# Layer 1 of a two-layer graph network: attention in fewer, larger interleaving steps, masks copied by ScalarE

## The chip, the cores and the metric

The kernel runs on one core of one Trainium2 chip. The metric is the device time in microseconds from the first to the last instruction of one execution. A core has five engines that run their own queues in order and meet at semaphores: TensorE (PE for matmuls, PEld for its weight loads), VectorE (DVE), ScalarE (ACT), GpSimd (POOL) and SyncE (SP, which here only starts transfers). Matmul results land in PSUM[...]; everything else lives in SBUF.

## The reference

32 graphs of 512 nodes with 256 features pass two layers, each a graph part and a feed-forward part with a layer norm ahead and a residual around it. Only layer 1's graph part is touched by the change. With `adj` of zeros and ones it is a four-head attention over the neighbours:

```python
h = jnp.einsum('bnd,hde->bhne', nodes_embed, W)
e_src = jnp.einsum('bhne,hte->bhtn', h, a_src)
e_dst = jnp.einsum('bhne,hte->bhtn', h, a_dst)
...
weight = weight + mask * (e_src[:, :, t, :, None] + e_dst[:, :, t, None, :])
weight = jax.nn.leaky_relu(weight, negative_slope=0.01)
weight = jnp.where(node_adj[:, None] == 0, NEG, weight)
attention = jax.nn.softmax(weight, axis=-1)
dst = jnp.einsum('bhij,bhje->bhie', attention, h) + bias[None, :, None, :]
out = jax.nn.relu(dst) + h
```

then a layer norm per head over 64 features. Its feed-forward part soft-assigns the nodes to 64 slices per head, runs a small bidirectional state-space mixer (`_hydra`) over the 64 slice tokens, and spreads the result back to the nodes.

## The kernel before

**Layer 0** (`layer0_sorted`, up to about 2540 us) does its graph convolution and feed-forward part. Near its end it already runs the first lines of layer 1: constants, and the masks of sequence 0 (L1093).

**Layer 1** (`layer1_plain`, L850) has two streams of work, both written as Python generators whose `yield` ends a step.

- The *attention* stream, `attentions` (L1292): for each sequence `b` it interleaves `attention(b)` with `prepare(b + 1)` through `woven` (L65), which takes steps of the two in proportion to the counts it is given.
- The *mixer* stream, `mixer` (L1557), for a pair of sequences: `slices` twice (logits `lgp` L1319, `exp` and the soft assignment `sw` on ScalarE and VectorE L1320 to L1326, the gathered tokens `yTp` L1331, the transposes `swp` L1336), `tokens`, `scan` (the state-space chain, `xp` L1384 to `vp` L1541), and `unslice` twice (`outp` L1551, added to `x` at L1553).

Each `yield` of the mixer names a wish (4, 7, 2 ...; 68 for a pair), and the loop at L1575 gives the attention stream `want * PACE` steps of credit for it. `PACE` (L881) follows from `TURNS` (steps of `attention`) and `STEPS` (steps of `prepare`). `slices` also pulls the attention stream until its own sequence has been attended (L1305). The order of these steps is the order in which instructions are given out; the framework plans each engine's queue from it.

`prepare(b)` gathers the rows (L1139), makes the mask (`masks`, L1058), normalises (`normed`), transposes (`turned`), projects each tile of 128 nodes (`hp`, L1165) with three exponentials and a copy on ScalarE (L1168 to L1171), adds the bias on GpSimd (L1174), and sends the nodes' own terms through DRAM to get them broadcast over partitions (`own`, L1185). A mask of one tile is made in `turn` (L1066): four bf16 transposes into a PSUM tile `maskp` and one copy to uint8 (L1070). Outside the start-up these PSUM tiles share a pool of four banks (`any`) with `hp`, `lgp`, `yTp`, `swp`, `outp` and the scan; four more banks (`pv`) hold the attention's sums.

`attention(b)` runs over four tiles `j` of neighbours and two head pairs `q`. A turn `(q, j)` is: `weigh` two turns ahead, that is two VectorE instructions L1198 (maximum of two exponentials, times the mask) into the `att` buffers; two matmuls `avp` (L1231), whose two heads stand side by side in TensorE's columns; and, when `q` is the second pair, four matmuls `adp` (L1238) for the softmax's denominators. Each turn ends a step. In between, pieces of `norm(b - 1)` (L1266), the head-wise layer norm of the sequence before, are run as steps of their own (L1241). At the end the sums are copied, transposed and divided (L1246 to L1261).

Of the kernel before, what the change touches and what calls it, by code (L numbers as in the profile page):

```python
# [18 lines left out]
P = 128  # L19
N = 512  # L20
D = 256
NT = N // P
# [42 lines left out]
def woven(a, na, b, nb):  # L65

    done_a = done_b = 0
    a, b, end = iter(a), iter(b), object()
    while a is not None or b is not None:
        if b is None or (a is not None and done_a * nb <= done_b * na):  # L70
            done_a += 1
            if next(a, end) is end:
                a = None
        else:
            state = next(b, end)
            if state is end:
                b = None
            elif state is True and a is not None:

                if next(a, end) is end:  # L80
                    a = None
            elif state is True:
                yield True
                continue
            if state is not True:
                done_b += 1
        yield
# [9 lines left out]
def layer0_sorted(tc, ident, eps, x, adj, w, x2s, ranks, over, following):  # L97
# [13 lines left out]
    CAPS = [24, 9, 7, 6, 5, 5, 5] + 5 * [4] + 4 * [3] + 7 * [2] + 9 * [1]  # L111
    STEPS = [16, 12, 9, 8, 7, 6, 5, 4, 3, 2, 1, 0]
    NC = len(STEPS)
    LEAD = 16
# [735 lines left out]
def layer1_plain(tc, ident, eps, x2s, ranks, adj, w, out, over, ps):  # L850
# [3 lines left out]
    nc = tc.nc  # L854
# [16 lines left out]
    SLOPE = 0.01  # L871
    HE = HO + 1
    AP = AH // 2
    TURNS = AP * NT + 6
    STEPS = 15
    WANTED = 68
    AHEAD = 2
    ATT = 2 * (AHEAD + 2) + AP + 1
# [1 line left out]
    AHEAD_X = 2 * GB + 1  # L880
    PACE = 1.04 * GB * (TURNS + STEPS) / WANTED  # L881

# [3 lines left out]
    with ExitStack() as ctx:  # L886
# [169 lines left out]
        masked = {}  # L1056

        def masks(b, bank="any"):  # L1058

            a, raw = [], []  # L1060

            def load(t):
                raw.append(se.tile([P, N], I32, tag="ai", name=f"ai{b}_{t}", bufs=2))
                nc.sync.dma_start(raw[t], adj[b, t * P : (t + 1) * P, :])

            def turn(t):  # L1066
                pt = ps.tile([P, NT, P], BF16, tag=bank, name=f"maskp{b}_{t}")
                for j in range(NT):
                    nc.tensor.transpose(pt[:, j, :], a[t][:, j * P : (j + 1) * P], identb)
                nc.vector.tensor_copy(mask[:, :, t * P : (t + 1) * P], pt)  # L1070

            load(0)
            load(1)
            yield
            for t in range(NT):
                n = b * NT + t
                a.append(se.tile([P, N], BF16, tag="a", name=f"a{b}_{t}", bufs=3))
                nc.scalar.activation(a[t], raw[t], AF.Identity, accum_out=edges[:, 0, n : n + 1])
                nc.scalar.activation(raw[t], raw[t], AF.Square, accum_out=edges[:, 1, n : n + 1])
                if t + 2 < NT:  # L1080
                    load(t + 2)
                if t == 1:
                    mask = se.tile([P, NT, N], mybir.dt.uint8, tag="mask", name=f"mask{b}")
                    yield
                if t > 1:
                    turn(t - 2)
                    yield
            for t in range(NT - 2, NT):
                turn(t)
                yield  # L1090
            masked[b] = mask

        yield from masks(0, "mm")  # L1093
# [39 lines left out]
        def prepare(b):  # L1133

            while b >= AHEAD_X and b - AHEAD_X not in stored:
                yield True
            xt = xs[b] = sb.tile([P, NT, D], F32, tag="x", name=f"x{b}", bufs=AHEAD_X)
            for t in range(NT):
                nc.gpsimd.indirect_dma_start(  # L1139
                    out=xt[:, t, :], out_offset=None, in_=x2s[b // SEG],  # L1140
                    in_offset=bass.IndirectOffsetOnAxis(
                        ap=ranks[:, b * NT + t : b * NT + t + 1].bitcast(U32), axis=0))

            hv = sb.tile([P, NT, AH, HE], F32, tag="hv", name=f"hv{b}")
            xn = hv.rearrange("p t h e -> p (t h e)")[:, : NT * D].rearrange("p (t d) -> p t d", t=NT)
            edged = masks(b) if b not in masked else range(3)
            for i, _ in enumerate(edged):
                if i < 3 or b not in masked:
                    yield
                if i == 2:  # L1150
                    normed(xt, xn, f"c{b}")
                    nc.gpsimd.tensor_add(xt, xt, beta.unsqueeze(1).to_broadcast([P, NT, D]))
                    yield
            mask = masked.pop(b)
            xnT = yield from turned(xn, "x3T", f"x3T{b}")
            yield


            ht = sb.tile([P, NT, AH * HO], F32, tag="ht", name=f"ht{b}")
            other = sb.tile([P, NT, AH], F32, tag="other", name=f"other{b}")  # L1160
            mine = sb.tile([P, AH, NT], F32, tag="mine", name=f"mine{b}")
            for t in range(NT):
                ph = psum("any", f"hp{b}_{t}")
                for c in range(DC):
                    nc.tensor.matmul(ph[:, : AH * (HO + 2)], xnT[:, c, t * P : (t + 1) * P], wa[:, c, :],  # L1165
                                     start=c == 0, stop=c == DC - 1)
                d = ph[:, AH * HO : AH * HO + AH]
                nc.scalar.activation(mine[:, :, t], ph[:, AH * (HO + 1) : AH * (HO + 2)], AF.Exp, scale=1.0 - SLOPE)  # L1168
                nc.scalar.activation(hv[:, t, :, HO], d, AF.Exp)
                nc.scalar.activation(other[:, t, :], d, AF.Exp, scale=SLOPE - 1.0)  # L1170
                nc.scalar.copy(ht[:, t, :], ph[:, : AH * HO])  # L1171
                yield

            nc.gpsimd.tensor_add(hv[:, :, :, :HO], ht.rearrange("p t (h e) -> p t h e", h=AH),  # L1174
                                 abias.rearrange("p (h e) -> p h e", h=AH).unsqueeze(1).to_broadcast([P, NT, AH, HO]))
            yield
            pt = psum("any", f"minep{b}")
            nc.tensor.transpose(pt[: AH * NT, :P], mine.rearrange("p h t -> p (h t)"), ident)
            row = sb.tile([AH * NT, P], F32, tag="turned", name=f"turned{b}", bufs=1)
            nc.scalar.copy(row, pt[: AH * NT, :P])  # L1180
            own_row = dr.tile([AH, N], F32, tag="own", name=f"ownd{b}")
            nc.sync.dma_start(own_row.rearrange("h (t p) -> (h t) p", p=P), row)
            own = [wide("own", f"own{b}_{h}", AH + 2) for h in range(AH)]
            for h in range(AH):
                nc.sync.dma_start(own[h], own_row[h].partition_broadcast(P))  # L1185
            for t in range(NT):
                nc.vector.tensor_mul(hv[:, t, :, :HO], hv[:, t, :, :HO], hv[:, t, :, HO:].to_broadcast([P, AH, HO]))
            ready[b] = mask, ht, hv, other, own
            yield
# [11 lines left out]
        def attention(b):  # L1201

            mask, ht, hv, other, own = ready[b]
# [19 lines left out]
            for i, (q, j) in enumerate(turns):  # L1223
                if i + AHEAD < len(turns):
                    begin(b, i + AHEAD)
                elif b + 1 in ready:
                    begin(b + 1, i + AHEAD - len(turns))

                for k in range(2):
                    h = 2 * q + k  # L1230
                    nc.tensor.matmul(pv[q][k * HO : (k + 1) * HO, :], hv[:, j, h, :HO], weighed[b, h, j],  # L1231
                                     start=j == 0, stop=j == NT - 1)

                if q + 1 == AP:
                    if j == 0:
                        pd = psum("pv", f"adp{b}")
                    for h in range(AH):
                        nc.tensor.matmul(pd[h * HW : (h + 1) * HW, :], hv[:, j, h, HO:].to_broadcast([P, HW]),  # L1238
                                         weighed.pop((b, h, j)), start=j == 0, stop=j == NT - 1)
                yield  # L1240
                if unfinished and i != 2:  # L1241
                    next(unfinished[0], None)
                    yield
                    if i > 2:
                        unfinished.pop()
            dT = wide("att", f"adT{b}", ATT)  # L1246
            nc.scalar.copy(dT, pd)
            vT = [wide("att", f"avT{b}_{q}", ATT) for q in range(AP)]
# [15 lines left out]
        unfinished = []  # L1264
# [27 lines left out]
        def attentions():  # L1292
            yield from prepare(0)
            for b in range(B):
                nxt = prepare(b + 1) if b + 1 < B else iter(())
                yield from woven(attention(b), TURNS - 4, nxt, STEPS)
            for _ in unfinished[0]:
                yield

# [924 lines left out]
```

## Time and profile before

The time before is 4619.27 us (median of 3, 4611.98 to 4620.72); the profiled execution spans 4621.6 us.

| engine | busy us | share of the span | instructions |
|---|---|---|---|
| PE (matmuls) | 4067.9 | 88% | 19287 |
| PEld (weight loads) | 2525.4 | 55% | 19287 |
| DVE | 3379.1 | 73% | 7040 |
| ACT | 2291.7 | 50% | 4756 |
| POOL | 1729.5 | 37% | 2027 |

In groups of instructions a line gives line, engine and operation, output and inputs by name, shapes and count, then busy time, the mean duration in ns, the idle time of the engine just before, and what ended it. In lists of waits, "A <- B: total, times, longest" means that A's engine stood idle until B. A timeline row gives start, duration, engine, line, operation and count; square brackets hold idle time ahead of it. Matmul durations overlap[...], so the distance from one start to the next is what a matmul costs. A matmul in f32 shows as two instructions, so `avp` x4 is two heads. The share of busy time is an average: layer 0 and layer 1 have different limits, and so have parts of a pair of sequences in layer 1.

### The profile page before, as it was taken

What the parts mean: (1) busy time and instruction counts of PE and PEld (TensorE: products, weight loads), DVE (VectorE), ACT (ScalarE), POOL (GpSimd) and SP (SyncE); (2) the same over time, 40 slices, a digit from 0 to 9 for tenths busy, and PEclk for the clock granted to TensorE, in tenths of its full rate; (3) what the DMA queues carried; (4) which work ended last, traced back from release to release, by engine and by line L of the source; (5) the groups of instructions that cost most, each with busy time, mean ns of one, the idle gap of its engine ahead of it and who ended that gap; (6) DMA issues with size and microseconds to landing.
All of it is one profiled execution on the core that took longest, in us unless ns stands there. A gap on an engine that the chain in (4) does not pass through costs nothing. (4 is left out here: it accounts for less than half of the span.)

```text
span 4621.6 us, 56127 instructions
## 1 busy us (share of the span) xinstructions
PE 4067.9 (88%) x19287; PEld 2525.4 (55%) x19287; DVE 3379.1 (73%) x7040; ACT 2291.7 (50%) x4756; POOL 1729.5 (37%) x2027
## 2 busy tenths in 40 slices
PE   5768898988988889888897899999999999999987
PEld 4545655656556566555554355555555555555555
DVE  6678778887788877777775777777787777777763
ACT  2344555545655556555564444545544454454432
POOL 2356444653435534353332223222323323332220
PEclk8889999999999999998998999999999999999998
DMA  5556433653436533374431111111111111111100
GB/s 125 172 158 214 164 127 126 198 178 124 136 118 198 177 129 112 99 263 145 141 115 48 53 46 56 51 48 44 44 54 49 56 56 53 47 54 56 40 14 15
DMA packets 235100, 474.09 MB, mean 103 GB/s; under 512 B 38299, under 2 KB 114075, under 8 KB 234804
## 3 DMA queue, kind: packets, MB, share of 16 engines
q0 software_dynamic: 80256, 282.38, 19.3%
q1 hardware_dynamic: 154548, 188.02, 13.3%
q8 instruction: 154, 2.52, 0.2%
q14 instruction: 142, 1.16, 0.1%
HBM read 413.16 MB, written 57.16 MB: 102 GB/s over the span
## 5 line engine op out<-in xcount | busy, mean ns | idle before, releaser
L609 PE MATMUL clsp<-xnT,wc 128*128 128x512 f32 x1024 | 512.1, 621 | 77.3 <-ACT cls L611 63.0
L609 PE MATMUL gatep<-xnT,wg 128*128 128x512 f32 x1024 | 497.7, 605 | 16.0 <-ACT gate L611 13.2
L638 PE MATMUL po<-wd,acc 128*128 128x256 f32 x2048 | 450.9, 381 | 0.4 <-DVE acc L627 0.3
L638 PEld LDWEIGHTS po<-wd,acc 128*128 128x128 f32 x2048 | 391.4, 191 | 65.9 <-issue 13.8
L422 PE MATMUL pm<-h,adj 128*128 128x257 f32 x1024 | 295.5, 435 | 136.3 <-DVE xs L640 67.3
L589 DVE SCALAR_TENSOR_TENSOR best<-rows,xs,best 128x1024 f32<-128x1024 f32 x212 | 276.1, 1305 | 165.4 <-ACT best L583 98.1
L623 DVE SCALAR_TENSOR_TENSOR acc<-past,fld,acc 128x512 f32<-128x512 f32 x448 | 351.1, 787 | 54.3 <-ACT past L622 45.5
L1198 DVE SCALAR_TENSOR_TENSOR att<-own,other,mask 128x512 f32<-128x512 f32 x512 | 378.9, 762 | 11.5 <-DMA own<-ownd 11.0
L586 POOL DMA_INDIRECT rows<-table,xs x212 | 261.1, 1232 | 237.3 <-DVE best L589 171.8
L609 PEld LDWEIGHTS gatep<-xnT,wg 128*128 128x128 f32 x1024 | 195.8, 195 | 260.5 <-issue 197.0
L622 ACT ACTIVATE past<-tz,fld 128x512 f32<-128x512 f32 x448 | 291.0, 694 | 83.4 <-DVE acc L623 83.0
L618 ACT ACTIVATE acc<-tz,fld 128x512 f32<-128x512 f32 x256 | 199.5, 779 | 265.1 <-PE tz L616 262.0
L422 PEld LDWEIGHTS pm<-h,adj 128*128 128x128 f32 x1024 | 212.4, 218 | 194.5 <-issue 106.7
L1231 PE MATMUL avp<-att,hv 128*64 128x512 f32 x1024 | 310.3, 628 | 4.2 <-DVE att L1198 4.2
L609 PEld LDWEIGHTS clsp<-xnT,wc 128*128 128x128 f32 x1024 | 185.7, 197 | 222.3 <-issue 121.1
L1331 PE MATMUL yTp<-sw,x 128*128 128x512 f32 x512 | 242.7, 614 | 39.8 <-DVE sw L1326 32.3
L611 ACT ACTIVATE cls<-clsp,fld 128x512 f32<-128x512 f32 x256 | 176.7, 690 | 201.7 <-PE clsp L609 86.9
L1319 PE MATMUL lgp<-wsl,x4T 128*128 128x512 f32 x512 | 252.0, 628 | 27.9 <-DVE mask L1070 21.7
L1139 POOL DMA_INDIRECT x<-x2s,ranks x128 | 140.9, 1101 | 343.0 <-DVE att L1198 104.1
L1284 POOL TENSOR_TENSOR mu<-mu,eps 128x16 f32<-128x16 f32 x32 | 121.3, 3791 | 324.2 <-DVE mu L1283 323.1
L611 ACT ACTIVATE gate<-gatep,fld 128x512 f32<-128x512 f32 x256 | 175.6, 686 | 127.5 <-PE gatep L609 103.6
L541 POOL DMA_INDIRECT xs<-rows_of,order x128 | 143.4, 1121 | 250.7 <-DVE acc L623 78.7
(597 smaller groups left out, 8961.5 us busy)
## 6 DMA issues: line engine op xcount, KB each, us to landing
adji<-in_adj SPq DMA_DIRECT2D x128, 256.0 KB
ai<-in_adj SPq DMA_DIRECT2D x128, 256.0 KB
own<-ownd SPq DMA_DIRECT2D x128, 256.0 KB
rows_of<-keep SPq DMA_DIRECT2D x32, 550.0 KB
x<-in_x SPq DMA_DIRECT2D x32, 512.0 KB
x2s<-xs SPq DMA_DIRECT2D x32, 512.0 KB
out<-x SPq DMA_DIRECT2D x32, 512.0 KB
rows<-table,xs POOLq DMA_INDIRECT x212
```

Of the source, the lines that this page charges most:

```text
L422: nc.tensor.matmul(pm[:, : D + 1], a[:, i, t * P : (t + 1) * P], h[:, i, :], start=i == 0, stop=i == NT - 1)
L586: nc.gpsimd.indirect_dma_start(out=row, out_offset=None, in_=table, in_offset=bass.IndirectOffsetOnAxis(ap=idxs[:, k : k + 1].bitcast(U32) ...
L589: nc.vector.scalar_tensor_tensor(m, row, vals[:, k : k + 1], m, ALU.add, ALU.max)
L609: nc.tensor.matmul(pf, wf[:, c, f * P : (f + 1) * P], xnT[:, c, :], start=c == 0, stop=c == DC - 1)
L611: nc.scalar.activation(o, pf, fn, bias=fld[:, f, bf : bf + 1], scale=1.0 if fn == AF.Gelu else 0.5)
L622: nc.scalar.activation(r, z, AF.Relu, bias=fld[:, f, AT + b : AT + b + 1])
L623: nc.vector.scalar_tensor_tensor(y, r, fld[:, f, CH + b : CH + b + 1], y, ALU.mult, ALU.add)
L638: nc.tensor.matmul(po[:, i, :], acc[f][:, t * P : (t + 1) * P], wd[:, f, :], start=f == 0, stop=f == FC - 1)
L1198: nc.vector.scalar_tensor_tensor(e, own[h], other[:, j, h : h + 1], mask[:, j, :], ALU.max, ALU.mult)
L1231: nc.tensor.matmul(pv[q][k * HO : (k + 1) * HO, :], hv[:, j, h, :HO], weighed[b, h, j], start=j == 0, stop=j == NT - 1)
L1319: nc.tensor.matmul(pf, xnT[:, c, t * P : (t + 1) * P], wsl[:, c, :], start=c == 0, stop=c == DC - 1)
L1331: nc.tensor.matmul(py, xn[:, t, c * P : (c + 1) * P], sw[:, t, :], start=t == 0, stop=t == NT - 1)
```

## The change

A step of the attention now holds a whole tile of neighbours (both head pairs, then the denominators); a step of `prepare` holds two tiles' projections or two tiles' masks. The pieces of `norm` run inside the attention's steps for tiles 0, 1 and 2. `TURNS` goes from 14 to 7, `STEPS` from 15 to 11, and the counts given to `woven` from 10 and 15 to 5 and 11. The mask's copy out of PSUM moves from VectorE to ScalarE. The arithmetic is the same. The aim is fewer changes between kinds of matmul on TensorE, and a lighter VectorE.

```diff
-    TURNS = AP * NT + 6
-    STEPS = 15
+    TURNS = NT + 3
+    STEPS = 11
...
-                nc.vector.tensor_copy(mask[:, :, t * P : (t + 1) * P], pt)
+                nc.scalar.copy(mask[:, :, t * P : (t + 1) * P], pt)
...
                 if t > 1:
                     turn(t - 2)
-                    yield
+            yield
             for t in range(NT - 2, NT):
                 turn(t)
-                yield
+            yield
             masked[b] = mask
...
-            edged = masks(b) if b not in masked else range(3)
+            edged = masks(b) if b not in masked else range(2)
             for i, _ in enumerate(edged):
-                if i < 3 or b not in masked:
-                    yield
-                if i == 2:
+                yield
+                if i == 1:
                     normed(xt, xn, f"c{b}")
                     nc.gpsimd.tensor_add(xt, xt, beta.unsqueeze(1).to_broadcast([P, NT, D]))
                     yield
...
                 nc.scalar.copy(ht[:, t, :], ph[:, : AH * HO])
-                yield
+                if t % 2:
+                    yield
...
                     for h in range(AH):
                         nc.tensor.matmul(pd[h * HW : (h + 1) * HW, :], hv[:, j, h, HO:].to_broadcast([P, HW]),
                                          weighed.pop((b, h, j)), start=j == 0, stop=j == NT - 1)
-                yield
-                if unfinished and i != 2:
-                    next(unfinished[0], None)
+                    if unfinished:
+                        next(unfinished[0], None)
+                        if j == 2:
+                            unfinished.pop()
                     yield
-                    if i > 2:
-                        unfinished.pop()
...
-                yield from woven(attention(b), TURNS - 4, nxt, STEPS)
+                yield from woven(attention(b), TURNS - 2, nxt, STEPS)
```

## The prediction

> **What bounds the kernel now.** I read the table of busy time by stretches first, because layer 1, the only part that changes, starts near 2540 us and runs to the end. Its columns are the length of the stretch, then busy time and instruction count of PE, PEld, DVE, ACT and POOL, the granted clock, the DMA share and GB/s:
>
> ```profile
> 3400.00:3600.00 200.00, 188.99 (x1172) 108.61 (x1171) 148.19 (x311) 100.11 (x255) 56.31 (x41) 0.98 0.14 43
> 3600.00:3800.00 200.00, 190.18 (x1023) 107.17 (x1020) 149.31 (x312) 93.98 (x243) 65.26 (x48) 0.98 0.19 59
> 4400.00:4621.00 221.00, 180.34 (x1043) 118.71 (x1043) 105.88 (x246) 75.04 (x160) 23.67 (x17) 0.88 0.05 15
> ```
>
> TensorE is the bound: over the nine stretches from 2600 to 4400 it is busy 1685.7 of 1800 us, VectorE 1335.8 (74%), ScalarE 870.1 (48%). So 114 us of TensorE idle there, plus the tail, is all that better feeding can win; the rest must come from TensorE's own work. The waits of TensorE from 2600 to 4400 (us in total, times, longest) say who causes the idle:
>
> ```profile
> PE yTp L1331 <- DVE sw L1326: 32.3, 26, 1.8
> PE lgp L1319 <- DVE mask L1070: 21.7, 6, 4.4
> PE maskp L1069 <- DVE mask L1070: 12.4, 7, 3.0
> PE oTp L1519 <- ACT yT L1513: 11.5, 14, 1.3
> PE yTp L1331 <- DVE sst L1325: 6.7, 2, 3.4
> ```
>
> VectorE causes 73 of the 85 us shown, the mask copy alone 34: it holds one of four PSUM buffers that `lgp` and `maskp` wait for. The timeline shows where, once per pair of sequences, just after the `outp` matmuls:
>
> ```profile
> 3497.30 5.37 PE L1319 MATMUL lgp<-wsl,x4T 128*128 128x512 f32 x12
> 3504.77 0.68 DVE L1070 CAST mask<-maskp 128x512 uint8<-128x512 bf16 x1
> 3505.50 0.59 PE L1069 MATMUL maskp<-identb,a 128*128 128x128 bf16 x4 [2.84 <-DVE mask L1070]
> 3513.86 4.56 PE L1331 MATMUL yTp<-sw,x 128*128 128x512 f32 x10 [1.77 <-DVE sw L1326]
> ```
>
> In the answering stretch of the pair before, 3366 to 3396, VectorE is busy 26.6 of 30 us and TensorE idle 4.3. A pair lasts 126.2 us (its first `outp` starts at 2719.76 and, 13 pairs on, at 4359.79), with 114/1800 x 126.2 = 8.0 us of idle; more than half falls in this stretch, where VectorE is briefly the bound. All four mask copies of a sequence run in it.
>
> The costs, from the groups of instructions from 2450 on (busy us, mean ns of one; the copy of `yT` stands in for the new mask copy):
>
> ```profile
> L1198 DVE SCALAR_TENSOR_TENSOR att<-own,other,mask 128x512 f32<-128x512 f32 x512 | 378.9, 762 | 11.5 <-DMA own<-ownd 11.0
> L1070 DVE CAST mask<-maskp 128x512 uint8<-128x512 bf16 x124 | 83.7, 678 | 5.5 <-PE maskp L1069 5.5
> L1332 ACT COPY yT<-yTp 128x512 f32<-128x512 f32 x64 | 37.5, 586 | 244.7 <-PE yTp L1331 244.7
> ```
>
> And what changing between kinds of matmul costs, from TensorE's timeline: in the first four rows each `avp` stands alone, the last two rows are a whole tile of neighbours at once.
>
> ```profile
> 3405.53 1.08 PE L1231 MATMUL avp<-att,hv 128*64 128x512 f32 x4
> 3406.53 3.70 PE L1319 MATMUL lgp<-wsl,x4T 128*128 128x512 f32 x8
> 3411.99 1.08 PE L1231 MATMUL avp<-att,hv 128*64 128x512 f32 x4
> 3413.00 1.06 PE L1238 MATMUL adp<-att,hv 128*32 128x512 f32 x8
> ...
> 4440.31 1.94 PE L1231 MATMUL avp<-att,hv 128*64 128x512 f32 x8
> 4442.18 1.06 PE L1238 MATMUL adp<-att,hv 128*32 128x512 f32 x8
> ```
>
> From start to the next start, one head pair takes 1.00 to 1.01 us, two pairs together 1.87. So joining two saves about 0.15 us.
>
> **What the skill says.** (1) The Trainium skill, "TensorE: Matmul & The Clock Gate", section "Single matmul latency", gives a lone matmul a constant of about 166 ns that a stream hides; the 0.15 us per join agrees. (2) "ScalarE: Activation LUTs", section "What ACT_TABLE_LOAD costs": a copy without pointer operands takes 186 + 0.833 N ns, 612 ns for N = 512 as an estimate; the trace has 586, which I use. No run here has a bf16 PSUM source with a uint8 target on ScalarE, so 0.59 is the nearest row; I allow 0.55 to 0.70. (3) The same page, section "Table sets: the hidden batching unit", puts copy in every set, so no table load (1283 ns here) is added; the copies of `yT` agree. (4) "Perfetto Trace Analysis", section "Optimization Strategy", says that consistent bubbles can mean that the next tile found no SBUF or PSUM; the 34 us behind the mask copy are that.
>
> **The change, part by part.**
>
> *Mask copies.* 128 copies leave VectorE: 128 x 0.68 = 87 us, 2.7 us per sequence, and in the stretch above all 2.7 count. ScalarE gains 128 x 0.59 = 75 us and goes from 48 to about 52%: hidden by its idle, of which single pieces last 15 us (`x4T` waiting). The new wait: a copy stands in ScalarE's queue until TensorE has done the transposes; behind it are `exp` of `lgp` (L1320) and the two passes over the next `ai`. Since those also follow TensorE's order, I charge 0 to 1 us per pair. Expected: of the 34 us, 20 to 30 vanish.
>
> *Whole tiles of neighbours.* An attention sequence has 7 steps for 14, and both head pairs' `avp` are given out together, then the `adp` of that tile. From 2541 on I count 201 lone `avp` pairs in TensorE's timeline and 41 longer runs. Up to 100 joins x 0.15 = 15 us, and as many interruptions of other matmuls removed (`lgp` x4 takes 1.82, x8 3.53, so 0.11 each): 11 us more. Together at most 26; some joins are broken again, so I take 17.
>
> *Two tiles' projections, two masks.* `hp` takes 1.00 us alone and 2.03 for two, `maskp` 0.24 and 0.54: nothing by themselves, at most 0.1 us for each of some 64 interruptions saved; I take 3.
>
> *Order and pace.* Per pair of sequences the steps wanted fall from 2 x (14+15+2) = 62 to 2 x (7+11+2) = 40 (each interleaving uses two more, to find each stream finished). The credit falls from 68 x 0.887 = 60.3 to 68 x 0.551 = 37.4. The shortfall, made up in one burst ahead of the second sequence, grows from 1.7 of 62 steps (2.7%) to 2.6 of 40 (6.4%). Worked through step by step, for most pairs the step that writes `own` moves from ahead of `vp` to about the second `unslice`. In the trace before, VectorE does ten L1198 instructions (7 us) under `outp`, when it has little else: that needs `own`. The way through DRAM took 3.9 to 4.7 us in the chain of waits. Moved later, four to eight of these (3 to 6 us) fall into the stretch where VectorE binds, and so does more of the first third of `norm` (L1274 to L1278, up to 4 us). Out of it go 2.7 us of mask copies and the second third of `norm` (L1282 to L1285, 3 us), which now follows the last `lgp`. Balance -5.7 + 3 to 10, so -2.7 to +4 us per pair; but TensorE has four tiles' `lgp` and two tiles of `avp` to put in front of a late `att`. I take +0.3, 5 us over 16 pairs. The planned order is not the text's order (L1198 runs between the adds of L1553 of one loop), so this can't be known closer.
>
> Sum: -25 - 17 - 3 + 5 = -40 us, or 4619 - 40 = 4579. I leave the tail as it is: from 4465 on only the last pair's chain runs, in both.
>
> **Rivals.**
> - *Feeding fully cured.* With VectorE near 70%, most of the 73 us behind it vanish and the joins hold: -60 - 30 = -90, 4529. For: all four copies lie in the bound stretch. Against: `sw` remains a chain of four VectorE operations per tile.
> - *Waits change name.* `lgp` and `yTp` wait for `sw` or `att` instead of the mask; only some 12 us of joins remain: 4607 to 4618, say 4612. For: VectorE at 26.6 of 30 us, and late `own`.
> - *Coarse steps starve TensorE: slower.* Late `own` puts 4 us more per pair on VectorE in the bound stretch, 16 x 4 = 64, with -20 from joins: 4663. For: the shortfall of 6.4% and three larger lumps (`att` x8, `norm`, two masks) on an in-order engine. Against: VectorE's idle of 26% and the lighter load.
>
> **How the numbers follow.** My forecast (4555 to 4605) gets 0.44, the full cure 0.16, waits changing name 0.17, starving 0.23. Of the third, two parts in three lie within 0.2% (4610 to 4628.5), one part below. Faster 0.44 + 0.16 + 0.06 = 0.66, the same 0.11, slower 0.23. The range 4530 to 4645 cuts half of the cure (0.08) and half of the starving (0.12), which includes the ends of the copy's price (128 x 0.15 us, hidden) and of the balance per pair.
>
> **What would show it.** In the profile after: no mask copy on VectorE, 128 on ScalarE near 0.59; no TensorE wait on `mask` L1070 worth more than 10 us; `avp` mostly in runs of 8 at 1.87; TensorE idle per pair near 6 us for 8.0; ten L1198 under `outp` reduced. I am wrong if `avp` waits for `att` by tens of us, if `lgp` waits for ScalarE's mask copy, or if `yTp` waits for `sw` by clearly more than 39 us from 2600 to 4400.

## The result, and the profile after

After the change the kernel takes 4764.66 us (median; 4761.01 to 4773.73), beside 4618.99 us before: a ratio of 1.0321 [1.0303, 1.0339], slower by 146 us. The prediction said 4579 us, range 4530 to 4645, faster.

The table of busy time by stretches, in the columns of the prediction, shows layer 1 after. The first row is the stretch in which all pairs are alike, the next two stand where the prediction showed two, the last is the tail:

```profile
2700.00:4400.00 1700.00, 1520.63 (x8586) 906.25 (x8581) 1103.05 (x2354) 796.46 (x2015) 461.22 (x351) 0.93 0.15 47
3400.00:3600.00 200.00, 174.34 (x902) 96.48 (x900) 120.23 (x254) 92.91 (x243) 56.22 (x43) 0.91 0.17 51
3600.00:3800.00 200.00, 177.94 (x1068) 107.74 (x1069) 139.73 (x295) 97.91 (x234) 50.32 (x36) 0.91 0.13 42
4538.00:4759.00 221.00, 173.99 (x1031) 113.77 (x1027) 98.98 (x230) 75.81 (x159) 22.35 (x15) 0.88 0.05 15
```

The same 1700 us of the kernel before:

```profile
2700.00:4400.00 1700.00, 1593.33 (x9423) 925.22 (x9421) 1257.18 (x2649) 823.40 (x2113) 509.88 (x376) 0.98 0.17 51
```

TensorE's idle time in the stretch grows from 107 to 179 us and its granted clock falls from 0.98 to 0.93, while VectorE, the engine that the change was to relieve, is less busy. Fewer matmuls fit into the same time (8586 for 9423). From one pair's first `outp` to the next pair's, 13 pairs take 138.1 us each for 126.2. By the shares of the two stretches that is 14.6 us of idle and 123.5 of busy TensorE in a pair, for 7.9 and 118.3. The tail is not longer than before.

TensorE's waits from 2600 to 4540 of the kernel after (total, times, longest) have other names than before:

```profile
PE yp L1495 <- DVE mix L1488: 39.6, 13, 4.3
PE avp L1231 <- DVE sst L1324: 38.7, 7, 5.9
PE yTp L1330 <- DVE sw L1325: 35.3, 19, 3.7
PE yTp L1510 <- DVE mu L1282: 28.6, 8, 3.6
```

The mask is gone from the list, as forecast. At its head stand two waits inside the scan (`yp` for `mix`, and `yTp` for `y`: `mu` L1282 is only the instruction after `y`), and `avp` waiting for its `att` (`sst` L1324 is only the instruction after it), which the prediction named as a sign of failure. In the kernel before, the scan's two waits were small; from 2600 to 4400, the stretch of the prediction's list, which leaves them out, they are:

```profile
PE yTp L1511 <- DVE y L1506: 6.7, 8, 0.9
PE yp L1496 <- DVE mix L1489: 4.3, 4, 2.0
```

The groups of instructions from 2450 on show that the mask copies cost what was forecast (0.60 us for 0.59) and that the attention's L1198 on VectorE hardly got longer (769 ns for 762):

```profile
L1198 DVE SCALAR_TENSOR_TENSOR att<-own,other,mask 128x512 f32<-128x512 f32 x512 | 370.6, 769 | 18.3 <-DMA own<-ownd 17.0 <-PE adp L1238 1.2
L1070 ACT CAST mask<-maskp 128x512 uint8<-128x512 bf16 x124 | 70.6, 603 | 21.0 <-PE maskp L1069 21.0
L1331 ACT COPY yT<-yTp 128x512 f32<-128x512 f32 x64 | 37.4, 584 | 246.5 <-PE yTp L1330 246.1
```

And the joins came about: counted from TensorE's timeline from 2541 on, `avp` runs of eight went from 29 to 75 and lone ones (x4) from 150 to 20.

**Where the time is lost** is seen best in one stage: the scan from `gp` (L1471 before, L1470 after) to the transposes of `y`. In the mean of the 13 pairs TensorE's idle time grows by 7 us (7.7 to 14.7), and 4.6 of them are in this stage (1.3 to 5.9). Of the rest, 1.9 us lie between the two sequences' slices, most of it before transposes that wait for ScalarE (`x` L1118), and 2.1 in the second sequence's slices (1.2 to 3.3), where `yTp` waits for `sw`. In a pair of the kernel before, VectorE's queue holds little there but the chain itself: sums of `mix`, its product with the decay, then, after `qp`, three steps of `y`. These are rows of the two engines' timeline:

```profile
3959.75 0.46 PE L1471 MATMUL gp<-cpad,bcT 64*64 64x64 f32 x8
...
3963.52 0.69 DVE L1488 TENSOR_TENSOR mix<-mix,back 128x512 f32<-128x512 f32 x1
3964.31 0.69 DVE L1489 TENSOR_TENSOR mix<-mix,decay 128x512 f32<-128x512 f32 x1
3965.15 1.87 PE L1496 MATMUL yp<-xk,mix 64*64 64x64 f32 x32
...
3969.30 0.69 DVE L1505 TENSOR_TENSOR y<-y,yp 128x512 f32<-128x512 f32 x1
3970.02 0.69 DVE L1506 TENSOR_TENSOR y<-y,z 128x512 f32<-128x512 f32 x1
3970.76 0.66 PE L1511 MATMUL yTp<-ident,y 128*128 128x128 f32 x4 [0.87 <-DVE y L1506]
```

It takes 11.0 us. The same rows of a pair after:

```profile
4048.59 0.45 PE L1470 MATMUL gp<-cpad,bcT 64*64 64x64 f32 x8
...
4055.39 0.68 DVE L1487 TENSOR_TENSOR mix<-mix,back 128x512 f32<-128x512 f32 x1
4055.99 1.22 DVE L1273 SCALAR_TENSOR_TENSOR av<-av,ht 128x1024 f32<-128x1024 f32 x1
4057.12 0.69 DVE L1488 TENSOR_TENSOR mix<-mix,decay 128x512 f32<-128x512 f32 x1
...
4057.96 3.27 PE L1495 MATMUL yp<-xk,mix 64*64 64x64 f32 x32 [3.72 <-DVE mix L1488]
...
4064.07 0.69 DVE L1504 TENSOR_TENSOR y<-y,yp 128x512 f32<-128x512 f32 x1
4066.45 1.22 DVE L1281 TENSOR_REDUCE mu<-ht 128x16 f32<-128x1024 f32 x1 [1.69 <-ACT ht L1279]
4067.58 0.68 DVE L1505 TENSOR_TENSOR y<-y,z 128x512 f32<-128x512 f32 x1
...
4068.41 1.09 PE L1510 MATMUL yTp<-ident,y 128*128 128x128 f32 x4 [3.58 <-DVE mu L1282]
```

It takes 19.8 us. Pieces of the layer norm (L1273 to L1281) stand between the chain's instructions, and so do the two multiplications that close the attention (L1258, 0.69 us each). The worst is L1281: it waits 1.69 us for ScalarE's squares and then runs 1.22, and `y` times `z`, whose inputs are there at 4064.8, starts only after it: VectorE runs its queue in order. The two stretches show what it does to TensorE (busy 9.72 of 11.01 us, then 11.58 of 19.82) and to its clock (1.00, then 0.69):

```profile
3959.75:3970.76 11.01, 9.72 (x84) 7.35 (x80) 5.69 (x12) 9.38 (x34) 3.67 (x5) 1.00 0.15 48
```

```profile
4048.59:4068.41 19.82, 11.58 (x96) 9.62 (x93) 14.84 (x29) 13.72 (x30) 3.67 (x4) 0.69 0.06 14
```

TensorE also had somewhat less other work here: averaged over the 13 pairs, matmuls that do not belong to the scan fill 6.0 us of this stage before and 5.4 after, the latter at a lower clock. That is too little to explain the longer stage by itself.

### The profile page after: what moved, and what is told of

The parts are those of the page before. It is cut to its first block, busy times and chain, and to the rows that moved or that the text cites. A ratio compares the mean times of both kernels' runs of the same rounds, so it can differ in the third digit from the quotient of the medians.

```text
span 4759.1 us, 56038 instructions
## 1 busy us (share of the span) xinstructions
PE 4115.8 (86%) x19287; PEld 2586.5 (54%) x19287; DVE 3304.5 (69%) x6912; ACT 2353.4 (49%) x4884; POOL 1720.4 (36%) x2027
## 4 chain that ended last, share of the span: by engine, by line
PE 37%; DVE 22%; POOL 12%; issue 11%; DMA 8%; ACT 5%; SPq 0%; POOLq 0%; DVEq 0%; ACTq 0%
PE clsp L609 4%; PE gatep L609 4%; PE yTp L1330 3%; PE outp L1550 3%; PE avp L1231 3%; DMA rows<-table,xs 3%; DVE acc L623 2%; PE pm L422 2%; POOL mu L1283 2%; PE po L638 2%; POOL rows L586 2%; PE hp L1164 2%; DVE best L589 2%; DMA rows<-table,tops 1%; POOL best L552 1%
## 5 line engine op out<-in xcount | busy, mean ns | idle before, releaser
L638 PEld LDWEIGHTS po<-wd,acc 128*128 128x128 f32 x2048 | 390.3, 191 | 66.9 <-issue 13.9
L1198 DVE SCALAR_TENSOR_TENSOR att<-own,other,mask 128x512 f32<-128x512 f32 x512 | 370.6, 769 | 18.3 <-DMA own<-ownd 17.0
L1231 PE MATMUL avp<-att,hv 128*64 128x512 f32 x1024 | 306.8, 629 | 53.4 <-DVE sst L1324 38.7
L609 PEld LDWEIGHTS clsp<-xnT,wc 128*128 128x128 f32 x1024 | 186.8, 198 | 226.8 <-issue 125.7
L1318 PE MATMUL lgp<-wsl,x4T 128*128 128x512 f32 x512 | 241.6, 618 | 2.5 <-issue 1.4
L625 DVE TENSOR_TENSOR acc<-acc,cls 128x512 f32<-128x512 f32 x256 | 186.4, 729 | 61.2 <-ACT acc L618 59.2
```

The lines of the kernel that those rows point to most:

```text
L609: nc.tensor.matmul(pf, wf[:, c, f * P : (f + 1) * P], xnT[:, c, :], start=c == 0, stop=c == DC - 1)
L638: nc.tensor.matmul(po[:, i, :], acc[f][:, t * P : (t + 1) * P], wd[:, f, :], start=f == 0, stop=f == FC - 1)
L1198: nc.vector.scalar_tensor_tensor(e, own[h], other[:, j, h : h + 1], mask[:, j, :], ALU.max, ALU.mult)
L1318: nc.tensor.matmul(pf, xnT[:, c, t * P : (t + 1) * P], wsl[:, c, :], start=c == 0, stop=c == DC - 1)
```

## The experiments

| kernel | median us | ratio to before [95%] |
|---|---|---|
| e1 before + masks by ScalarE | 4601.86 | 0.9965 [0.9955, 0.9975] |
| e2 whole change, masks by VectorE | 4739.34 | 1.0270 [1.0247, 1.0294] |
| e3 before + attention's whole tiles | 4792.66 | 1.0375 [1.0350, 1.0400] |
| e4 before + merged `prepare` | 4616.76 | 0.9993 [0.9980, 1.0006] |
| e5 change, faster pace | 4714.40 | 1.0208 [1.0186, 1.0230] |
| e6 change, head pairs apart | 4656.73 | 1.0089 [1.0073, 1.0106] |
| e7 change, norm in steps of its own | 4741.34 | 1.0269 [1.0252, 1.0286] |
| e8 change without the attention's part | 4607.12 | 0.9975 [0.9967, 0.9982] |
| e9 change, `own` a step earlier | 4737.83 | 1.0273 [1.0251, 1.0295] |
| e10 before, no norm | 4578.66 | 0.9922 [0.9902, 0.9943] |
| e11 change, no norm | 4606.81 | 0.9983 [0.9974, 0.9992] |
| e12 change, `own` earlier, no norm | 4648.31 | 1.0070 [1.0053, 1.0087] |
| e13 e1 + 4 instructions in the chain | 4663.93 | 1.0115 [1.0099, 1.0130] |
| e14 e1 + the same 4 outside it | 4598.64 | 0.9960 [0.9945, 0.9976] |
| e15 change, norm held back | 4742.99 | 1.0279 [1.0264, 1.0293] |

### Which part of the change loses the time

e1 makes the mask's edit alone:

```diff
-                nc.vector.tensor_copy(mask[:, :, t * P : (t + 1) * P], pt)
+                nc.scalar.copy(mask[:, :, t * P : (t + 1) * P], pt)
```

e2 is the whole change without that edit. e3 makes only the attention's edit (with its `TURNS` and `woven` counts), e4 only that of `prepare` (with `STEPS`), e8 that of `prepare` and the masks.

> The kernel before, with nothing but the mask copies moved to ScalarE. Theory 1 (the whole-tile attention steps are what costs: matmuls of the attention are all spent early and the state-space chain of the mixer is left without other work to cover it) expects 4580 to 4620 us, since the copy leaves VectorE where it binds. Theory 2 (ScalarE's queue, held up by copies that wait for TensorE, is what costs) expects 4700 or more. Theory 3 (the merged steps of prepare, with the own terms sent later, are what costs) expects as theory 1.

> The kernel after, with the mask copies back on VectorE. Theories 1 and 3 expect 4765 to 4810 us: VectorE gets its 87 us of copies back and the coarse steps stay. Theory 2 expects about 4620 to 4660.

> The kernel before, with only the attention's steps made a whole tile of neighbours (7 for 14, the pieces of norm inside them); prepare in 15 steps and mask copies on VectorE as before. Theory 1 expects 4720 us or more, that is two thirds or more of the loss of 146 us. Theory 3 expects 4600 to 4650. Theory 2 expects about 4620.

> The kernel before, with only the steps of prepare merged (11 for 15: two projections, two masks); attention in 14 steps and mask copies on VectorE as before. Theory 1 expects 4600 to 4650 us. Theory 3 expects 4720 or more. Theory 2 expects about 4620.

> The change without its attention part: prepare's steps merged and the masks copied by ScalarE, attention in 14 steps as before. If the attention's steps are the whole loss, whatever it is in them, 4590 to 4615 us, that is the gain of the mask copies (15 us alone) with nothing lost. If merged masks on ScalarE hold up its queue only together, 4625 or more.

The attention's whole tiles alone are slower than the whole change (4793); the two other parts together gain 12 us (4607), the masks alone 15 (4602), the merged `prepare` nothing. So the loss comes with one part. In e1 TensorE is busier than before in the same stretch from 2700 to 4400, at a clock of 0.99:

```profile
2700.00:4400.00 1700.00, 1599.45 (x9413) 922.98 (x9412) 1195.18 (x2575) 873.78 (x2225) 502.62 (x376) 0.99 0.17 51
```

But the parts don't add up: added to the finely stepped kernel the masks by ScalarE gain 15 us, added to the other two parts they lose 25 (e2 to the change). The order of VectorE's and TensorE's queues is planned anew in each kernel, and it differs in more places than the edit. e2 also came out below the 4765 to 4810 that was expected; why it is the better of the two stays open. It is not that its scan is clear: TensorE is idle for 6.2 us a pair there.

### What of the whole tiles: grain, pace, norm, own

e6 ends a step after each head pair again, and leaves the norm's pieces inside the second one. e7 keeps the whole tile and gives each piece of the norm its own step (both with the counts of `woven` to match). e5 raises the pace so that the shortfall is that of before.

```diff
# e6: TURNS = AP * NT + 3
-                    yield
+                yield
# e7: TURNS = NT + 6
+                    yield
-                    if unfinished:
+                    if unfinished and j < 3:
...
-                    yield
+                        yield
# e5
-    PACE = 1.04 * GB * (TURNS + STEPS) / WANTED
+    PACE = 1.081 * GB * (TURNS + STEPS) / WANTED
```

> The kernel after, with the pace factor at 1.081 for 1.04. The interleaving uses two steps more per sequence than the pace counts, so before the attention got 1.04 x 29/31 = 0.973 of the steps that it needs, and after it 1.04 x 18/20 = 0.936; 1.081 x 18/20 gives 0.973 again. Theory A (the attention falls behind more and is made up in bursts) expects 4600 to 4670 us. Theory B (two head pairs in one step) and theory C (norm's pieces inside the attention's steps) expect 4740 to 4790.

> The kernel after, with every head pair's turn a step of its own again (8 + 3 steps for 4 + 3), while norm's three pieces stay inside the steps of tiles 0, 1 and 2, and prepare and masks stay as after. Theory B expects 4590 to 4660 us. Theory C and theory A expect 4720 or more.

> The kernel after, with norm's three pieces as steps of their own again (4 + 3 + 3 steps for 4 + 3), while a step still holds a whole tile of neighbours, and prepare and masks stay as after. Theory C expects 4590 to 4660 us. Theory B and theory A expect 4720 or more.

Smaller steps recover 108 of the 146 us (4657, inside 4590 to 4660), the pace 50 (4714, between the ranges of both theories), separate norm steps only 23 (4741). e6 and e7 change the pace too, as it follows from the steps: by the sum that e5's text makes, the attention gets 0.95 of the steps that it needs in both, for 0.936 in the change. So the pace does not tell the two apart. In e6, from 2600 to 4540, neither of the scan's two waits is left at any size, `yp` on `mix` 8.8 us and `yTp` 4.1 in all; what remains is `lgp` waiting for ScalarE's `x4T`:

```profile
PE lgp L1318 <- ACT x4T L1128: 61.8, 11, 7.0
PE yTp L1330 <- DVE sw L1325: 32.2, 32, 1.8
```

e6 also shows that the scan is not the only place. It differs from e8 only in that the norm has no steps of its own (and in the counts), its scan is clear of the norm in all but the last full pair, and it is still 50 us slower than e8 (4657 for 4607). Where the norm goes costs time elsewhere too, by the list ahead of the logits; no run followed this up.

e7's small gain spoke against the norm, since it does move the norm out of the scan (0.9 us a pair from `gp` to `yTp`, for 4.6 after). But the wait for `y` stayed:

```profile
PE yTp L1511 <- DVE y L1506: 53.4, 14, 4.2
```

The timeline of e7 shows why. Another VectorE instruction, L1187 of `prepare`, has come to stand in the norm's place, and it is stretched from 0.42 to 1.98 us while GpSimd works:

```profile
3509.28 2.54 POOL L1312 TENSOR_TENSOR x<-x,outb 128x1024 f32<-128x1024 f32 x1 [0.58 <-ACT x L1118]
3509.53 0.68 DVE L1505 TENSOR_TENSOR y<-y,yp 128x512 f32<-128x512 f32 x1
3510.13 1.98 DVE L1187 TENSOR_TENSOR hv<-hv 128x256 f32<-128x256 f32 x1
3512.03 0.68 DVE L1506 TENSOR_TENSOR y<-y,z 128x512 f32<-128x512 f32 x1
```

e9 makes and sends `own` right after the last `hp`, one step earlier, in answer to `avp <- sst`: in one of the pairs where `own` is late, the transposes `minep` that it comes from start at 4096.55, 13.9 us after the first `outp` (before: 4.0 us ahead of it), and `avp` stands in TensorE's queue ahead of logits that could run:

```profile
4099.76 3.60 PE L1318 MATMUL lgp<-wsl,x4T 128*128 128x512 f32 x8
4109.08 3.21 PE L1231 MATMUL avp<-att,hv 128*64 128x512 f32 x4 [5.72 <-DVE sst L1324]
4112.22 2.08 PE L1318 MATMUL lgp<-wsl,x4T 128*128 128x512 f32 x2
```

```diff
# e9: the nine lines from pt = psum("any", f"minep{b}") to the dma_start of own[h], moved up
                nc.scalar.copy(ht[:, t, :], ph[:, : AH * HO])
+                if t == NT - 1:
+                    pt = psum("any", f"minep{b}")
...
                if t % 2:
                    yield
```

> The kernel after, with the own terms sent (transposed, copied, and through DRAM) in the step of the last projections, one step of prepare earlier, in front of the bias addition on GpSimd; all else as after. In the trace of after this transpose runs 7 to 14 us behind the first outp matmul, before it ran 4 us ahead of it. Theory D (in the pairs where it runs behind all outp matmuls, att comes late and TensorE waits 5.3 to 5.9 us for it, at a low clock afterwards) expects 4690 to 4725 us and no wait of avp over 3 us. If it is nothing by itself, 4745 or more.

4738, 27 us recovered, where 4690 to 4725 was expected: `avp` no longer waits, but that was a fifth of the loss.

e10, e11 and e12 leave out the head-wise layer norm (L1275 to L1286 of after; L1273 and the addition of the attention's result to `x` stay) from before, from the change, and from e9:

```diff
# e10, e11, e12: in norm
-            nc.vector.tensor_reduce(mu[:, 0, :], heads, AX.X, ALU.add)
...
-            nc.vector.tensor_mul(heads, heads, mu[:, 1, :].unsqueeze(2).to_broadcast([P, NG, HO]))
```

> The kernel before, without the head-wise layer norm of the attention: mean, variance, power and the scaling are left out, the addition of the attention's own value and the residual stay, and so do the steps. It takes some 8 us of VectorE per sequence away (seven instructions of 128 x 1024 or their like). A base for the next two: 4540 to 4600 us, since TensorE stays the bound.

> The kernel after, without the head-wise layer norm in the same way. Theory E (with coarse steps norm's long VectorE instructions stand in front of the mixer's chain of mix and y, and TensorE waits for those) expects that the loss of 146 us against the same kernel before shrinks to 70 us or less, what stays being theory D. If norm only happens to be there, the loss stays at 110 us or more.

> Both of these on the kernel after: no head-wise layer norm, and the own terms sent one step earlier. If theories D and E are the whole loss, within 25 us of the kernel before without norm. If a third part is in it, 60 us or more above.

Without the norm the change costs 28 us (4607 to 4579) instead of 146. So 118 us need the norm's instructions to come about, wherever they stand. But with `own` early and no norm the kernel is 42 us slower again (4648). That is 70 us above the kernel before without norm, where at most 25 was expected if `own` and the norm were the whole loss, and 60 or more if a third part is in it. Moving `own` has gained 27 us with the norm and lost 42 without it; why is left open.

### Whether it is the scan's chain

e13 to e15 ask whether what stands in VectorE's queue between `gp` and `yTp` sets the time. In e1 the planned order has no other VectorE instruction there in 14 of 16 pairs. e13 puts four in, which change no value; e14 puts the same four where TensorE never waits for them. e15 is the whole change, but holds the norm's pieces back from the second sequence's slices until `y` is made.

```diff
# e13
             nc.vector.tensor_add(mix, mix, back)
+            for _ in range(2):
+                nc.vector.tensor_tensor(mix, mix, mix, ALU.max)
...
             nc.vector.tensor_add(y, y, py)
+            for _ in range(2):
+                nc.vector.tensor_tensor(y, y, y, ALU.max)
# e14, in unslice ahead of the store
+            for _ in range(2):
+                nc.vector.tensor_tensor(xt[:, :2, :], xt[:, :2, :], xt[:, :2, :], ALU.max)
# e15, with held set ahead of the second slices and cleared after the yield behind y * z
-                    if unfinished:
-                        next(unfinished[0], None)
-                        if j == 2:
-                            unfinished.pop()
+                    if unfinished and not held[0] and next(unfinished[0], True):
+                        unfinished.pop()
```

> The kernel before with the masks copied by ScalarE, and four VectorE instructions more in each pair of sequences: twice mix = max(mix, mix) ahead of mix*decay, twice y = max(y, y) ahead of y*z. They change no value; each is 128x512 f32, 0.69 us, 2.8 us a pair, 44 us over 16 pairs, and they stand inside the scan's chain, between gp and yTp, where that kernel's VectorE does nothing else. Theory Q (the chain of VectorE instructions in the scan sets how long that stage lasts, since TensorE has only some 6 us of other work there; what stands in VectorE's queue between gp and yTp is paid for in full, also in a finely stepped order): 25 to 60 us more than masks by ScalarE alone, so 4627 to 4662, and TensorE's idle time between gp and yTp goes from 0.8 to 2.5 us or more a pair. Theory F (the steps' coarseness counts, because TensorE has no work at hand; 2.8 us of VectorE with 30% idle cost nothing in a fine order): within 12 us of 4602.

> The same four instructions of 0.69 us for each pair, but outside the chain: twice x = max(x, x) on half a sequence's tiles just ahead of the store of each sequence, which TensorE never waits for. Same VectorE load as in the run before. Theory Q: within 15 us of masks by ScalarE alone (4602). If VectorE's total load is what counts (theory L): as much more as with the chain loaded, 25 to 60 us.

> The whole change, but the pieces of the layer norm are not given out from the second sequence's slices until y has been made; they follow in the next attention steps. By the order of VectorE's queue, the stage from gp to yTp then holds pieces of the norm in 3 of 15 pairs (all but one or two in alternation before), the four multiplications L1187 in 4, and neither in the others. Theory Q: pairs with a clean queue there last 126 to 131 us, pairs with pieces of the norm 138 or more; in all 4670 to 4715. Theory F (coarse steps starve TensorE whatever stands in VectorE's queue): all pairs stay at 135 to 144 us, 4735 or more.

The pair of e13 and e14 is plain: 44 us of VectorE work cost 62 us inside the chain (4664, just above the 4627 to 4662 of theory Q) and nothing outside it (4599). A pair of sequences goes from 125.2 to 129.5 us in e13, 125.7 in e14. The kernel has the same fine steps and the same matmuls in both, so neither coarseness nor VectorE's load is needed for a loss: what stands in the chain is paid for. The wait for `y`, from 2600 to 4540, is the one that grew, in e1 and in e13:

```profile
PE yTp L1511 <- DVE y L1506: 11.8, 11, 4.8
PE yTp L1515 <- DVE y L1510: 54.6, 14, 9.2
```

The cost is a little more than the work put in. In 9 of 16 pairs `y` times `z` was pushed under one of GpSimd's long instructions and took 2.7 us instead of 0.69. These nine add 18 us of VectorE time to the 44, which makes up the 62:

```profile
4116.18 1.42 DVE L1509 TENSOR_TENSOR y<-y 128x512 f32<-128x512 f32 x2
4116.99 2.81 POOL L1174 TENSOR_TENSOR hv<-ht,abias 128x1024 f32<-128x1024 f32 x1 [3.10 <-ACT ht L1171]
4117.63 2.72 DVE L1510 TENSOR_TENSOR y<-y,z 128x512 f32<-128x512 f32 x1
```

The Trainium skill, "Trainium Architecture — The Big Picture", section "What this means for kernel authors", says that VectorE and GpSimd share a port pair under an exclusive lock; this agrees, with 2.0 us of stretch. In the kernel before such stretches add up to about as much (about 70 us from 2700 to 4440, after about 60), so they are not the loss; it matters which instruction they fall on.

e13 lengthens the chain itself; in the change, other work stands between its instructions, which the rows above show and e15 tries to undo.

e15 missed its total: 4743, where theory Q said 4670 to 4715 and theory F 4735 or more. Its pairs do differ much as theory Q said (126 to 131 us for clear ones; they last 128 to 134), and not as F said. By what VectorE's queue holds between `gm` and `y` times `z`, the time from one pair's first `outp` to the next is:

| kernel | pieces of the norm | L1187 | neither |
|---|---|---|---|
| before | | | 13 pairs: 126.2 |
| e1 | | | 13: 125.2 |
| e6 | | | 13: 130.2 |
| after | 8 pairs: 141.3 | | 5: 132.9 |
| e2 (masks by VectorE) | 12: 134.9 | | 1: 136.2 |
| e5 (faster pace) | 2: 144.4 | | 11: 132.4 |
| e9 (`own` early) | 8: 139.5 | | 5: 127.7 |
| e7 (norm apart) | 3: 138.3 | 10: 135.0 | |
| e15 (norm held) | 2: 144.0 | 4: 137.6 | 7: 130.4 |

The pairs of the first column hold the attention's closing multiplications there too, so their extra time is not the norm's alone. The chain is not all: e2 holds up to three pieces of the norm there in nearly every pair, and its pairs last hardly longer than the clear ones of the change and of e5; and e5's clear pairs, in which `avp` has no long wait either, are 7.2 us longer than e1's.

Over those 13 pairs e15 is 44 us faster than the change (134.7 for 138.1 us a pair). It gave 29 of them back ahead of the first pair (its first `outp` starts at 2732.6 us, after at 2703.3) and 6 in the last full one, so that 9 us are left between the two profiled executions (22 between the medians). Where neither the norm nor L1187 stands in the chain, pairs are shorter; but L1187 takes its place in four of them, and the start is delayed. The theory holds by the pairs, and the forecast of the total left out the start.

From the table the loss of 12.9 us a pair against e1 can be shared out, using e9 for what `own` does: pieces of the norm in the chain, (139.5 - 127.7) x 8/13 = 7.2 us; late `own`, 138.1 - 135.0 = 3.1 us; the rest, 127.7 - 125.2 = 2.5 us, is what pairs keep with neither. About as much as this rest is TensorE's idle time in the second sequence's slices, 1.2 us a pair before and 2.9 in e9, and still 3.0 without the norm in e11. By the change's own pairs alone, the norm's share is (141.3 - 132.9) x 8/13 = 5.2 us. These are comparisons of pairs within kernels whose order differs in other ways too (with e5's 132.4 for a clear pair the norm's share would be smaller still), so the shares are rough estimates. That loading the chain costs time is shown by e13; how much of the change's loss that is, is estimated.

## Why the prediction was wrong

**What bounds the kernel** was read rightly, as far as it went: TensorE is the bound and VectorE causes most of its idle time. But the stage that mattered was not looked at. The prediction followed the largest waits, after `outp`, and does not mention the scan's `yTp <- y` (6.7 us) and `yp <- mix` (4.3 us). They were small in an order that keeps that chain clear.

**Mask copies, -25 us:** direction right, too large. The copies left, took 0.60 us on ScalarE, and after the change no wait of TensorE on them is over 1.3 us. Alone they gain 15 us (e1); there `yTp` waits longer for `sw` (58.9 us from 2700 to 4400, for 32.3), which is part of the rival "waits change name".

**Whole tiles of neighbours, -17 us:** the joins came (75 runs of eight). Their gain can't be seen apart: the slower clock lengthens matmuls by more. The constant for a lone matmul that the prediction set beside its 0.15 us is stated for bf16 and `avp` is f32, so that the two numbers agree shows nothing.

**Merged `prepare`, -3 us:** e4 gives nothing, 0.9993 [0.9980, 1.0006].

**Order and pace: this is the step that failed.** "I take +0.3, 5 us over 16 pairs", from a balance of -2.7 to +4 us per pair. The pairs got 11.9 us longer in all, 12.9 beside e1. The balance counted VectorE's work in one stretch, after `outp`, and took time there as the price. It asked how much work moves, not what it would stand in front of. That stretch did not get worse: from a pair's first `outp` to the last `yTp` of its first sequence TensorE is idle for 3.5 us a pair after and 4.1 before: the mask's waits left it (2.5 us), and the late `avp` waits took their place (3.3). The moved pieces of the norm went into the scan, where TensorE waits at the end of VectorE's chain: its idle time there went from 1.3 to 5.9 us a pair. The step gave this wait no cost at all. The signs that the prediction named as refuting it were there: `avp` waits by tens of us (38.7 on `sst`).

**The rival "coarse steps starve TensorE"** had the side right and a chance of 0.23. Its reason, 4 us more on VectorE through late `own`, is the smaller part: e9 takes late `own` away and recovers 27 of 146 us. "Three larger lumps on an in-order engine", which it names in passing, is nearer to what the rows show (one of the three, the norm), and no time was given to it.

**The clock** was left out. Single `avp` matmuls after 5.72 us of idle take 1.06 to 1.12 us for 0.59 (the row of 3.21 us is longer still because its second head's `att` came later), and `yp` after 3.72 us takes 3.27 for 1.87. TensorE is busy 5.2 us longer a pair for the same matmuls. The Trainium skill, "TensorE: Matmul & The Clock Gate", section "Part 1: The HAM clock gate (the "warmup" mystery)", has the clock fall to half after an idle window of about 3.4 us. The trace agrees that it falls to half with both waits, which are longer than that (the granted clock is the third figure from the end):

```profile
4052.84:4056.25 3.41, 0.78 (x10) 0.41 (x7) 3.31 (x7) 3.41 (x10) 0.00 (x0) 1.00 0.13 11
4056.25:4073.32 17.07, 11.79 (x63) 10.51 (x64) 10.84 (x13) 9.49 (x30) 6.17 (x2) 0.50 0.16 53
4107.45:4114.27 6.82, 5.19 (x8) 1.13 (x8) 6.82 (x11) 0.00 (x0) 4.20 (x4) 0.50 0.20 58
```

But in the first case it falls 2.0 us after the last matmul has ended (4054.24), so it did not take 3.4 us of idle time there. So waits of this kind cost more than themselves: of the 11.9 us that a pair got longer, 6.7 are idle time and 5.2 slower matmuls.

What stays open: why moving `own` earlier loses 42 us without the norm, why the masks by ScalarE lose 25 us in the coarse order, what e6 loses beside e8 with a clear scan, and the 2.5 us a pair that stay with a clear chain and early `own`.

## What to carry to other kernels

On an in-order engine, ask of every piece of work that a new step size moves what it will stand in front of: here 2.8 us of VectorE put into the scan's chain cost 4.3 us a pair (1.1 of them by meeting GpSimd), and outside it nothing, at the same load. Small waits in a profile can be the result of an order that keeps a chain clear, so check the chains with little slack before merging steps, not only the largest waits. Here the part worth keeping is the mask's copy alone, 0.9965 [0.9955, 0.9975].

## What the runs showed of the hardware

A VectorE product of two 128x512 f32 tiles takes 0.69 us alone and 2.72 when it meets a GpSimd addition of 128x1024 f32; one of 128x256 goes from 0.42 to between 1.98 and 2.59. The stretched ones shown end 0.3 to 0.6 us after GpSimd's instruction, so they seem to be held until it has ended rather than to run slowly. `y` plus `yp`, which has one operand in PSUM, took 0.68 us under the same GpSimd instruction (the rows of e7). TensorE's mean clock in a stage of 20 us fell to 0.69 with waits of 3.7 and 3.6 us in it, and was 1.00 in the same stage with waits below 1 us. From 2700 to 4400 of the change all 32 stretches of half clock last one, two, four or five times 3.41 us.
